# Attention of layer 0: the sums of the keys turned by four transposes and added on VectorE, the last sample's outputs turned in another PSUM bank, and the second sample's input loaded three steps later

## The chip, the cores and the metric

The kernel runs on one core of a Trainium2 chip. The metric is the device time in microseconds. TensorE does the matmuls and transposes, VectorE and ScalarE (ACT in the profile, VectorE is DVE) the elementwise work, GpSimd (POOL) some setup, and SyncE (SP) issues most DMA transfers. [...]

## The reference

Two layers work on x of shape 4 x 128 x 64 x 64. Only layer 0 is touched by the change; layer 1 (an attention with eight heads over 4096 tokens and a layer of 64 experts) follows it in the same kernel.

```python
e1 = _conv1x1(x, w1, b1, a1).reshape(N, -1, HW)     # x is the group-normed input
e2 = _conv1x1(x, w2, b2, a2).reshape(N, -1, HW)
asm = _conv1x1(x, wa, ba, aa).reshape(N, C, HW)
score = jnp.einsum('nci,ncj->nij', e1, e2)
score = jax.nn.softmax(score, axis=2)
out = jnp.einsum('nij,ncj->nci', score, asm)
x = x + out
```

So for each of four samples there are 4096 queries and 4096 keys of 64 channels and values of 128 channels. All of it is fp32.

## The kernel before, in words

Layer 0 goes through the samples b, in each through eight blocks qb of 512 queries, and in each block through 16 steps p of two key chunks of 128. A list `steps` holds the 512 steps in order. `probs` of a step multiplies keys and queries into a PSUM tile `sc` (two buffers), has ACT write the exponentials `pr` (three buffers), and has VectorE add them into `acc`, which so collects, for each query, the sum over the keys of each partition. `weigh` multiplies `pr` with the values into two PSUM tiles `av`. The scores of a step are issued two steps ahead of its weighing.

Behind a block's last step comes its tail. `collect` adds the two `av` tiles into `o` and the two halves of `acc` into `sums` (a single buffer). The rest is done for the block before, called `done`: `row_sums` sums `sums` over the partitions, that is over the keys, with four small matmuls against a column of ones into the PSUM tile `pd`, copies the result to `rows` and takes the reciprocal `inv`; `finish` turns `o` by four transposes into the PSUM tile `otr`, and VectorE scales it with `inv`, adds the input `xr` and writes the tokens `t`. Between `row_sums` and `finish` TensorE gets other work: in samples 0 to 2 the projections (`project`, tile `pe`, and `value`, tile `pa`) of the next sample; in the last sample the transposes of layer 1's tokens (`tokens`, tile `f_ltr`, copied by ACT to `f_ama`) and, from block 1 to 6, layer 1's four key chunks (`keys`, tile `f_pk`). In the last sample some steps of layer 1's scan (tile `f_ur` and others) are put there too by `point()`.

PSUM tiles with the same tag share a bank: `pd` and `pa` use bank `sm`; `pe`, `f_ltr`, `f_ur` and `otr` use bank `x`. A tile in a bank waits until the readers of the tile before it have finished.

TensorE's instructions keep the order in which the program writes them. In layer 0 the order on VectorE, ACT, POOL and SP is decided when the program is built, by priorities and estimated times, so an operation written at one place can stand elsewhere in its engine's queue. The input of a sample, `x`, has a single buffer: the load of the second sample can start when the first sample's last normalization (`normal`) has read it. It consists of four transfers on SP, and the statistics (`stat`, line 1923) of the second sample read it. Those same queues carry, for each chunk of the projection, the transfers `e<-e` and `e<-side`, which TensorE's scores need.

`tile_stats` and `close_stats` take the LayerNorm statistics of the sample before on VectorE (lines 256 and 257) and its root on ACT (line 260).

## Time and profile before

| what | us |
|---|---|
| median of three runs | 2300.96 (2299.47 to 2301.77) |
| the profiled execution | 2302.78 |
| its span, from the first to the last instruction | 2301.0 |
| TensorE busy | 2237.1 |
| VectorE busy | 1448.4 |
| ACT busy | 1092.1 |
| POOL busy | 174.8 |

Layer 0 fills about the first 1530 us of the span. One step takes 2.57 us there; in the middle of a sample a block takes 44.9 us, in the last sample about 51.7. A line of the profile's timeline gives the start, the duration, the engine, the line of the source, the operation and its tiles, how many like instructions were merged, and in brackets how long the engine was idle before it and what ended that. PE is TensorE's matmuls, PEld its weight loads. An fp32 matmul is two records (two passes), a transpose is one.

### The profile page before, as it was taken

To read this page: it belongs to the slowest core of one execution; us is meant where nothing else is said; L and a number is where in the kernel's file an instruction comes from. 1 tells how busy PE (TensorE), PEld (TensorE's weight loads), DVE (VectorE), ACT (ScalarE), POOL (GpSimd) and SP (SyncE) were. 2 spreads that over 40 slices of the span, in tenths; PEclk is the share of its full clock that TensorE was granted. 3 is DMA by queue.
4 is the path that set the end of the run, shared out by engine and by line. 5 is a ranking of instruction groups with operands and counts; after the bars stand their busy time and mean duration, and the time that the engine had idled before them with its cause. 6 is when DMAs were issued, how large, how long until landed. Compare 5 with 4: busy or idle time off the path is not lost.

```text
span 2301.0 us, 43192 instructions
## 1 busy us (share of the span) xinstructions
PE 2237.1 (97%) x18352; PEld 1161.9 (50%) x18352; DVE 1448.4 (63%) x2380; ACT 1092.1 (47%) x1328; POOL 174.8 (8%) x380
## 2 busy tenths in 40 slices
PE   7999999999999999999999999999999999999997
PEld 3544444444444444444444444456556555666663
DVE  7666565655666565556555666567867777775643
ACT  2343334433333443344445454445566666565651
POOL 0000000000000000000000000021221221223311
PEclk9999999999999999999999999999999999999999
DMA  2100010000010000001000000010211211323588
GB/s 75 34 12 17 9 45 9 17 9 9 11 52 9 9 17 9 9 9 44 9 5 5 5 5 10 5 50 25 64 46 39 65 53 41 94 55 113 170 301 331
DMA packets 79419, 108.96 MB, mean 47 GB/s; under 512 B 9072, under 2 KB 44912, under 8 KB 78960
## 3 DMA queue, kind: packets, MB, share of 16 engines
q1 hardware_dynamic: 78128, 104.01, 14.5%
q8 instruction: 146, 2.39, 0.4%
q0 software_dynamic: 512, 1.05, 0.2%
q10 hardware_dynamic: 576, 1.05, 0.1%
q14 instruction: 57, 0.47, 0.1%
HBM read 80.64 MB, written 19.14 MB: 43 GB/s over the span
## 4 chain that ended last, share of the span: by engine, by line
PE 88%; DVE 6%; ACT 3%; DMA 2%; issue 1%; SPq 0%; ACTq 0%; DVEq 0%
PE av L2033 37%; PE sc L2008 18%; PE f_pv L1130 9%; PE f_pk L975 8%; PE f_pt L1153 3%; PE f_po L1176 2%; PE pd L2059 1%; PE f_po L1188 1%; ACT f_e1a L982 1%; PE pa L1981 1%; PE pe L1955 1%; DMA x<-in_x_dram 1%; DVE f_e1a L983 1%; DVE f_e1a L984 1%; PE f_pl L1296 1%
## 5 line engine op out<-in xcount | busy, mean ns | idle before, releaser
L2033 PE MATMUL av<-pr,am 64*128 64x512 f32 x4096 | 978.0, 592 | 1.9 <-ACT pr L2013 1.8
L2013 ACT ACTIVATE pr<-sc 128x1024 f32<-128x1024 f32 x512 | 524.2, 1024 | 781.2 <-PE sc L2008 767.7
L2020 DVE TENSOR_TENSOR acc<-acc,pr 128x1024 f32<-128x1024 f32 x480 | 586.7, 1222 | 485.4 <-ACT pr L2013 481.1
L2033 PEld LDWEIGHTS av<-pr,am 64*128 64x128 f32 x4096 | 401.7, 187 | 471.7 <-issue 458.0
L2008 PE MATMUL sc<-e,e 64*128 64x512 f32 x2048 | 534.7, 591 | 4.8 <-DMA e<-side 4.8
L2008 PEld LDWEIGHTS sc<-e,e 64*128 64x128 f32 x2048 | 201.6, 187 | 237.0 <-issue 229.2
L1130 PE MATMUL f_pv<-f_held,f_ama 128*32 128x256 f32 x4096 | 239.3, 382 | 6.2 <-ACT f_e1a L982 5.1
L975 PE MATMUL f_pk<-f_held,f_ama 128*128 128x512 f32 x512 | 235.0, 603 | 0.0
L1135 ACT ACTIVATE f_amb<-f_pv 128x1024 f32<-128x1024 f32 x128 | 131.0, 1025 | 132.3 <-PE f_pv L1130 131.3
L983 DVE TENSOR_TENSOR f_e1a<-f_e1a,f_held 128x1024 f32<-128x1024 f32 x128 | 157.6, 1232 | 47.8 <-ACT f_e1a L982 47.6
L982 ACT ACTIVATE f_e1a<-f_pk 128x1024 f32<-128x1024 f32 x128 | 129.8, 1025 | 110.0 <-PE f_pk L975 56.7
L1130 PEld LDWEIGHTS f_pv<-f_held,f_ama 128*32 128x32 f32 x4096 | 129.7, 110 | 101.7 <-issue 12.4
L984 DVE TENSOR_REDUCE f_e1a<-f_e1a 128x8 f32<-128x1024 f32 x128 | 155.3, 1218 | 3.5
L975 PEld LDWEIGHTS f_pk<-f_held,f_ama 128*128 128x128 f32 x512 | 92.5, 190 | 108.3 <-issue 101.0
L1094 POOL COPY f_held<-f_e1a 32x32 f32<-32x32 f32 x128 | 30.7, 240 | 911.1 <-DVE f_e1a L1076 565.8
L1153 PE MATMUL f_pt<-f_amb,f_held 128*32 128x128 f32 x1920 | 83.2, 276 | 0.8 <-ACT f_amb L1135 0.8
L920 POOL MEMSET f_held<- 128x1024 f32 x1 | 1.0, 957 | 1035.2 <-DVE xn L1946 1035.2
L1153 PEld LDWEIGHTS f_pt<-f_amb,f_held 128*32 128x32 f32 x1920 | 60.0, 109 | 10.4 <-issue 5.2
L1194 DVE TENSOR_TENSOR t<-t,f_po 128x512 f32<-128x512 f32 (+1 forms) x33 | 22.1, 672 | 56.0 <-PE f_po L1188 56.0
L958 ACT ACTIVATE f_xl<-t,ln_nb,ln_rs 128x128 f32<-128x128 f32 x128 | 52.8, 491 | 0.8 <-PE pa L1981 0.8
L1277 ACT ACTIVATE f_x<-t,f_gnb,f_grs 128x128 f32<-128x128 f32 x122 | 49.7, 482 | 0.4 <-DVE f_gnb L1256 0.4
L2017 DVE COPY acc<-pr 128x1024 f32<-128x1024 f32 x32 | 22.2, 694 | 39.3 <-ACT pr L2013 39.3
(304 smaller groups left out, 1792.9 us busy)
## 6 DMA issues: line engine op xcount, KB each, us to landing
f_e2a<-f_rd SPq DMA_DIRECT2D x128, 128.0 KB, 3.1
xr<-in_xtok_dram SPq DMA_DIRECT2D x32, 256.0 KB, 2.6
f_table<-f_x SPq DMA_DIRECT2D x62, 128.0 KB, 2.2
out_dram<-t SPq DMA_DIRECT2D x14, 512.0 KB, 5.0
x<-in_x_dram SPq DMA_DIRECT2D x12, 512.0 KB, 4.5
e<-e SPq DMA_DIRECT2D x32, 128.0 KB, 2.2
f_ama<-f_rd SPq DMA_DIRECT2D x16, 256.0 KB, 4.0
f_e1b<-f_rd SPq DMA_DIRECT2D x16, 256.0 KB, 3.9
```

The lines of the kernel that those rows point to most:

```text
L958: nc.scalar.activation(xl[:, c, :], t[:, b * NCH + i, :], AF.Identity, bias=ln_nb[:, b, i : i + 1], scale=ln_rs[:, b, i : i + 1],)
L975: nc.tensor.matmul(pk[:, i, :], xt_at(n)[:, bass.ts(c, P)], env.wks[:, bass.ts(i, BLK)], start=True, stop=True,)
L982: nc.scalar.activation(flat, pk.rearrange("p i x -> p (i x)"), AF.Silu)
L983: nc.vector.tensor_mul(ks, ks, env.qb)
L984: nc.vector.tensor_reduce(s[:, (n % GB) * CPB + c, :], ks, AX.X, ALU.add)
L1130: nc.tensor.matmul(pv[a * CH : (a + 1) * CH, i, :], xt_at(m)[:, bass.ts(c * NA + i, CH)], env.wvs[:, bass.ts(a, HH * C)], start=True, stop ...
L1135: nc.scalar.activation(env.amb[:, bass.ts(c, HD)], pv.rearrange("p i x -> p (i x)"), AF.Silu)
L1153: nc.tensor.matmul(env.pt[i * CH : (i + 1) * CH, :], lhs, rhs, start=i not in env.begun, stop=False, skip_group_check=True,)
L2008: nc.tensor.matmul(sc[:, u, :], e2[halves[u], p, :], e1[halves[u], cols], start=True, stop=True,)
L2013: nc.scalar.activation(pr, sc, AF.Exp)
L2020: nc.vector.tensor_add(acc, acc, pr)
L2033: nc.tensor.matmul(av, am[h, j, :], pr[h, u, :], start=(j == 0), stop=(j == NCH - 1))
```

## The change

`collect` is split: the addition of the two halves of `acc` becomes `add_keys`, which is called behind `row_sums` of the block before. `row_sums` turns the four 128-query parts of `sums` with transposes into a whole bank, and VectorE adds over the keys in one reduction. `finish` gets the tag of its PSUM tile as an argument: bank `sm` in the last sample, bank `x` otherwise and for the very last block. The load of the second sample is called at step 13 of the first block instead of at step 10, where the last chunk is projected.

```diff
                 def collect(b, qb):
                     lower, upper_ = av_of.pop((b, qb))
-                    o = tmp.tile([P, BLK], F32, tag="o", name=f"o_{b}_{qb}")
+                    o_of[b, qb] = o = tmp.tile([P, BLK], F32, tag="o", name=f"o_{b}_{qb}")
                     nc.scalar.copy(o, lower)
                     nc.vector.tensor_add(o, o, upper_)
+
+                def add_keys(b, qb):
+                    o = o_of[b, qb]
                     acc = acc_of.pop((b, qb))
                     sums = tmp.tile([P, BLK], F32, tag="sums", name=f"sums_{b}_{qb}", bufs=1)
                     nc.vector.tensor_add(sums, acc[:, 0, :], acc[:, 1, :])
...
                 def row_sums(b, qb):
...
-                    pd = ps.tile([P, BLK], F32, tag="sm", name=f"pd_{b}_{qb}")
+                    pd = ps.tile([P, CPB, P], F32, tag="sm", name=f"pd_{b}_{qb}")
                     for c in range(CPB):
-                        nc.tensor.matmul(
-                            pd[:, c : c + 1], sums[:, bass.ts(c, P)], ones, start=True, stop=True
-                        )
-                    nc.vector.tensor_copy(rows[:, at], pd[:, :CPB])
+                        nc.tensor.transpose(pd[:, c, :], sums[:, bass.ts(c, P)], ident)
+                    nc.vector.tensor_reduce(rows[:, at], pd, AX.X, ALU.add)
...
-                def finish(b, qb):
+                def finish(b, qb, tag="x"):
...
-                    ptr = ps.tile([P, CPB, C], F32, tag="x", name=f"otr_{b}_{qb}")
+                    ptr = ps.tile([P, CPB, C], F32, tag=tag, name=f"otr_{b}_{qb}")
...
-                        if k == NBLK - 1:
-                            xs_of[1] = load_x(1)
+                    if n == NPR - 3:
+                        xs_of[1] = load_x(1)
...
                         collect(b, qb)
                         if done:
                             row_sums(*done)
+                        add_keys(b, qb)
...
                         if done:
-                            finish(*done)
+                            finish(*done, "sm" if b == B - 1 else "x")
```

## The prediction

> **What bounds the kernel now.** I read the page's first part, then the chain of waits, the groups with shapes kept apart, the list of TensorE's waits in layer 0, and the timeline at several block ends.

> ```profile
> PE 2237.1 (97%) x18352; PEld 1161.9 (50%) x18352; DVE 1448.4 (63%) x2380; ACT 1092.1 (47%) x1328; POOL 174.8 (8%) x380
> PE 88%; DVE 6%; ACT 3%; DMA 2%; issue 1%; SPq 0%; ACTq 0%; DVEq 0%
> ```

> TensorE is busy 97% of the span and is 88% of the chain: an edit counts by what it adds to or takes from TensorE's own sequence. VectorE (63%) has room on average, but it is crowded just behind a block's end, where this change puts its work.

> ```profile
> L984 DVE TENSOR_REDUCE f_e1a<-f_e1a 128x8 f32<-128x1024 f32 x128 | 155.3, 1218 | 3.5
> ...
> L2059 PE MATMUL pd<-ones,sums 128*128 128x1 f32 x256 | 33.6, 252 | 0.0
> ...
> L2044 DVE TENSOR_TENSOR sums<-acc 128x512 f32<-128x512 f32 x32 | 22.2, 692 | 16.3 <-PE pd L2059 16.2
> ...
> L2071 PE MATMUL otr<-ident,o 128*128 128x128 f32 x128 | 19.7, 276 | 8.6 <-ACT f_ama L968 6.9 <-ACT y L1957 1.1 <-DVE f_e1a L995 0.6
> ```

> Columns: busy us, mean ns of one, idle before it and its cause. The four row-sum matmuls of a block are 8 records (256 for 32 blocks), its four transposes are 4. The means (252, 276) include latency that overlaps the next record, so cost is read from start to start in the timeline of one tail, the stretch between two blocks (T = 174.88, where pd starts):

> ```profile
> 174.88 1.05 PE L2059 MATMUL pd<-ones,sums 128*128 128x1 f32 x8
> ...
> 175.79 1.10 PE L1955 MATMUL pe<-xn,w 128*128 128x512 f32 x2
> 175.97 0.69 DVE L2044 TENSOR_TENSOR sums<-acc 128x512 f32<-128x512 f32 x1 [0.54 <-PE pd L2059]
> 176.58 0.15 DVE L2062 COPY rows<-pd 128x4 f32<-128x4 f32 x1
> ...
> 176.88 1.13 PE L1981 MATMUL pa<-was,xn 128*128 128x128 f32 x8
> ...
> 177.84 0.60 PE L2071 MATMUL otr<-ident,o 128*128 128x128 f32 x4
> ...
> 178.37 1.99 PE L2033 MATMUL av<-pr,am 64*128 64x512 f32 x8
> ```

> TensorE goes from pd to pe in 0.91 us (T+0.91), starts pa at T+2.00, otr at T+2.96 and the next av at T+3.49. The four otr transposes hold it 0.53 us. On VectorE the sums wait for pd to have read the old sums (16.2 us over the run), and pa, which takes pd's bank, starts just after the rows copy has ended (176.73).

> **What the change costs, part by part.**

> *Row sums by transposes (32 blocks).* Removed: 8 records, 0.91 us. Added: 4 transposes of otr's kind. I take 0.55 us (0.53 after pa; 0.58 in the row of 1221.50 below, where they start cold). So pe starts at T+0.55 and its two passes, 0.43 each, end at T+1.41. [...]

> *The sum on VectorE.* A 128x4 copy (0.155) becomes a reduction of 128x512 from PSUM, which the trace does not have. Nearest rows: o, 128x512 reading PSUM, 0.69; and L984, a reduction of 1024 elements in 1218 ns, no slower than the add of that size (1222). I take 0.69; bounds 0.6 and 1.2. It can start at T+0.70 (o, which ran from 174.74, ends T+0.55; the transposes' last record ends T+0.66), ends T+1.39, and pa follows 0.12 to 0.15 later as it now follows the copy: T+1.54 against T+2.00. **Gain of a plain tail: 0.46 us.** Otr's bank waits for y, which ends at T+2.4 (pe's end T+1.65 plus ACT's 0.69), as pa ends: covered, by almost nothing. VectorE's order changes too: reduction, acc, reciprocal, sums, instead of sums, copy, reciprocal, acc. Sums no longer wait for TensorE; acc needs the pr that ACT ends at T+1.13. By start spacings (0.61, 1.11, 0.16, 0.61) z begins at T+3.19 instead of T+3.09. VectorE is therefore 0.1 later in absolute time and 0.56 later against TensorE. Where a step's probabilities (3 buffers) are awaited with slack that costs nothing; behind z wait e, side, t, statistics and the next acc, and at five tails TensorE waits for one of these:
> - the tail at 126.4 with two projections (otr waited 1.1 us for y, which waited for VectorE's e): -0.1.
> - the two with an x load and its statistics (VectorE waits for the DMA until 324.4; av waits at 331.84): -0.1 each.
> - the two at 446 and 807, where the LayerNorm root stands between two exponentials on ACT. There the built order puts the acc addition ahead of the last aggregate instead of behind it (the order of VectorE's queue in both programs shows it):

> ```profile
> 455.03 0.30 DVE L257 BATCH_NORM_AGGREGATE ln_mv<-l_st 128x2 f32<-128x6 f32 x2
> 455.25 1.19 DVE L2020 TENSOR_TENSOR acc<-acc,pr 128x1024 f32<-128x1024 f32 x1
> 455.37 0.32 ACT L260 ACTIVATE ln_rs<-ln_mv,eps 128x32 f32<-128x32 f32 x1 [0.61 <-DVE ln_mv L257]
> ...
> 458.08 1.99 PE L2033 MATMUL av<-pr,am 64*128 64x512 f32 x8 [0.55 <-ACT pr L2013]
> ```

> The root waits for the aggregate, av (458.08) for the exponential after the root. Spacing 1.11 plus 0.1, less rounding: -1.15 each.

> Samples 0 to 2 have 23 such tails: 18 x 0.46 = 8.3, less 0.1, 0.2 and 2.3: **+5.7 us**.

> *Last sample's outputs in bank sm.* Now they share bank x with the tokens' transposes and wait until ACT has copied these out:

> ```profile
> 1219.65 0.60 PE L967 MATMUL f_ltr<-ident,f_xl 128*128 128x128 f32 x4
> ...
> 1220.86 0.58 ACT L968 COPY f_ama<-f_ltr 128x512 f32<-128x512 f32 x1
> ...
> 1221.50 0.66 PE L2071 MATMUL otr<-ident,o 128*128 128x128 f32 x4 [1.25 <-ACT f_ama L968]
> ...
> 1222.08 1.99 PE L2033 MATMUL av<-pr,am 64*128 64x512 f32 x8
> ```

> ```profile
> PE otr L2071 <- ACT f_ama L968: 6.9, 6, 1.2
> PE sc L2008 <- DMA e<-side: 4.8, 3, 2.1
> ```

> Otr could have started 0.44 after ltr, and started 1.85 after it: 1.40 lost. In bank sm it waits for the reduction instead, done 5 us earlier because four key chunks lie between. By block:
> - 0: TensorE gains 0.7, but pr of step 2 then comes behind a LayerNorm root that waits for t on VectorE: -0.1.
> - 1 to 4: 0.36 + 1.40 = 1.76 earlier; pr of step 2 ended 1.1 us before its use (1226.23, used 1227.34) and moves only 0.36 with the keys, so 0.35 comes back as a wait: 1.41 each, 5.6.
> - 5 (no normals on ACT there): 1.76.
> - 6: f_ur in bank x still waits for the copy; the wait behind it goes: 1.13.
> - 7: no keys lie between. Otr now waits for the reduction, which stands behind o on VectorE (1526.03 to 1526.72): ends 1527.34, otr at 1527.46 instead of 1526.22: -1.24. The final row sums, behind it: +0.33.

> Sum **+7.5 us**. POOL's setup waits for the last t, about 1.4 later; TensorE is 0.9 later there, and POOL is next needed at 1545: covered by 4 us.

> *The clock.* One stretch of 3.5 us at half clock stands right behind block 6's tail:

> ```profile
> 1479.60:1483.10 3.50, 1.66 (x13) 0.94 (x11) 3.45 (x5) 3.17 (x4) 0.00 (x0) 1.00 0.00 0
> 1483.10:1486.60 3.50, 3.50 (x10) 1.48 (x12) 3.50 (x7) 0.55 (x1) 0.00 (x0) 0.52 0.00 0
> ```

> The row of 1479.60 has TensorE busy 1.66 of 3.50 us; the next has the clock at 0.52. [...] Tails of 2.4 us without a matmul (blocks 1 to 5) drew no dip; this one, 3.4, did. With the change it is 2.6: **+1.7 us**. [...]

> *Second x loaded three steps later.* At no cost and no gain. The order of instructions on SP's queue is the same in both programs: the four x transfers still stand behind the sixth chunk's side transfer and ahead of the seventh chunk's e and side, waiting for the same VectorE step; the statistics of x stand at the same place on VectorE. No queue is passed; POOL's and SP's orders are identical. The 4.8 us that sc waits for e<-side stay.

> Sum: 5.7 + 7.5 + 1.7 = 14.9 us. The profiled execution took 2302.8 (span 2301.0, 1.8 around it): 2287.9, span 2286.1. The median shown, 2300.96, lies 1.8 below the profiled time; less 14.9 it is 2286. After 1531 TensorE is 98 to 99% busy until 2100 and the weights' loads start from rooms it frees, so the shift is carried to the end.

> **Rivals.**
> 1. *The bank is slow (no change).* The reduction takes 1.2 us, L984's figure. Then pa starts at T+2.05: 18 x -0.05; the five special tails -5.1; last sample +6.0; clock +1.7: gain 1.8, 2299. Serial transposes (1.10 us) end near 2301. For: no row reduces from PSUM. Against: o's 0.69 does read PSUM.
> 2. *VectorE's queue decides (slower).* One mechanism: the reduction holds bank sm before pa and stands ahead of acc. [...] It decides from about 1.25 us on. Against: nothing of 128x512 on VectorE takes over 0.7 here.
> 3. *The x load does move.* If its statistics leave the seventh chunk's path, the 4.8 us go as well: 2281. Against: identical orders.
> 4. *The change does little at the plain tails*, because y or z decide otr or the next steps: their 0.46 becomes 0.2: 2291. It is in the forecast's range.

> **Numbers.** Forecast with rival 4: 0.80, gains of 9 to 20. Rival 3: 0.06. Rival 1: 0.08, no change. Rival 2: 0.06. Within 0.2% (4.6 us) is about what a measurement of this kernel can't tell from no change. Faster 0.86, same 0.08, slower 0.06. Range 2280 to 2294: low end, transposes at 0.44 and no lag on ACT (+21); high end, rival 4 with no clock gain and one more lag of 1 us per root (+7); it leaves out rivals 1 and 2.

> **What would show it.** Right: pd's four records in 0.6 us, pe at T+0.55, reduction near 0.69, pa at T+1.5; otr's 6.9 us wait for f_ama gone, a new wait of about 1.2 for rows at block 7; longer av waits for pr (from 1.8 to about 5); no clock dip near 1480; e<-side still 4.8. Wrong: a reduction over 1 us, pa later than T+1.9, exponentials waiting for acc in every tail, or new half-clock stretches in layer 0.

## The result

| | before | after |
|---|---|---|
| median | 2301.36 us (2298.48 to 2303.56, 6 runs) | 2288.24 us (2285.81 to 2288.86, 6 runs) |
| ratio after to before | | 0.994, 95% interval 0.9929 to 0.995 |
| span of the profiled execution | 2301.0 | 2287.0 |
| TensorE busy | 2237.1 | 2223.4 |
| VectorE busy | 1448.4 | 1460.2 |

The changed kernel is faster by 13.1 us by the medians; 14.9 were forecast. The interval of the ratio means 11.5 to 16.3 us. The end of layer 0 (the last `pd`) comes at 1517.42 us instead of 1530.13, 12.7 us earlier, of the 14.0 by which the profiled span is shorter: nearly all of the gain is made in layer 0, where the change is.

First the page's busy times, then two of the edited lines from the groups with shapes kept apart (busy us, mean ns of one, idle before it and its cause), after the change:

```profile
PE 2223.4 (97%) x18224; PEld 1147.4 (50%) x18224; DVE 1460.2 (64%) x2380; ACT 1091.6 (48%) x1328; POOL 175.9 (8%) x380
```

```profile
L2063 DVE TENSOR_REDUCE rows<-pd 128x4 f32<-128x512 f32 x32 | 22.1, 692 | 7.1 <-PE pd L2062 2.7
...
L2072 PE MATMUL otr<-ident,o 128*128 128x128 f32 x128 | 19.4, 274 | 2.8 <-DVE rows L2063 1.8 <-ACT y L1957 1.0
```

TensorE has 128 records fewer, VectorE 11.8 us more. The reduction, which the trace of before did not have, takes 692 ns, as the forecast took from `o` (0.69). The outputs' transposes wait 2.8 us instead of 8.6, and no longer for `f_ama`. The chain of waits of this profile consists of one piece of 0.01 us and tells nothing; TensorE's share of the span, still 97%, stands for it here.

A plain tail in the timeline of the changed kernel (T = 176.61, the same tail that the prediction shows at 174.88):

```profile
176.61 0.66 PE L2062 MATMUL pd<-ident,sums 128*128 128x128 f32 x4
...
177.11 1.02 PE L1955 MATMUL pe<-xn,w 128*128 128x512 f32 x2
177.31 0.69 DVE L2063 TENSOR_REDUCE rows<-pd 128x4 f32<-128x512 f32 x1
177.91 1.22 DVE L2020 TENSOR_TENSOR acc<-acc,pr 128x1024 f32<-128x1024 f32 x1
...
178.05 1.16 PE L1981 MATMUL pa<-was,xn 128*128 128x128 f32 x8
...
179.05 0.60 PE L2072 MATMUL otr<-ident,o 128*128 128x128 f32 x4
...
179.58 1.99 PE L2033 MATMUL av<-pr,am 64*128 64x512 f32 x8
```

From `pd` to `pe` it is 0.50 us (0.91 before), `pa` starts at T+1.44 (T+2.00), `otr` at T+2.44 (T+2.96), the next `av` at T+2.97 (T+3.49). The reduction starts as the transposes end and ends at T+1.39; `pe` holds TensorE until about then as well (its two passes of 0.43 end at T+1.36), so there is next to nothing left between `pe` and `pa`.

In the last sample the tail that the prediction shows at 1219.65 now reads:

```profile
1215.92 0.60 PE L967 MATMUL f_ltr<-ident,f_xl 128*128 128x128 f32 x4
...
1216.36 0.60 PE L2072 MATMUL otr<-ident,o 128*128 128x128 f32 x4
...
1217.14 0.58 ACT L968 COPY f_ama<-f_ltr 128x512 f32<-128x512 f32 x1
```

`otr` follows 0.44 behind `f_ltr` instead of 1.85, ahead of the copy that it used to wait for. At the last block, where no key chunks lie between, it waits instead for the reduction, which stands behind `o`:

```profile
1512.15 0.69 DVE L2041 TENSOR_TENSOR o<-o,av 128x512 f32<-128x512 f32 x1 [1.75 <-ACT o L2040]
1512.75 0.68 DVE L2063 TENSOR_REDUCE rows<-pd 128x4 f32<-128x512 f32 x1
...
1513.49 0.66 PE L2072 MATMUL otr<-ident,o 128*128 128x128 f32 x4 [1.41 <-DVE rows L2063]
```

TensorE's waits in layer 0 (the first 1535 us; total us, times, longest) after the change:

```profile
PE av L2033 <- ACT pr L2013: 8.1, 10, 2.2
PE sc L2008 <- DMA e<-side: 3.9, 2, 2.1
...
PE otr L2072 <- DVE rows L2063: 1.8, 2, 1.4
```

The 6.9 us for `f_ama` are gone, 1.8 for `rows` are new. The waits of `av` for the exponentials grew from 1.8 to 8.1, more than the 5 foreseen. Half of the growth is at the two LayerNorm-root tails, where the wait is 2.15 instead of 0.55; this is the one at 805.17 (T):

```profile
814.25 1.19 DVE L2020 TENSOR_TENSOR acc<-acc,pr 128x1024 f32<-128x1024 f32 x1
...
815.36 0.17 DVE L257 BATCH_NORM_AGGREGATE ln_mv<-l_st 128x2 f32<-128x6 f32 x1
815.57 0.32 ACT L260 ACTIVATE ln_rs<-ln_mv,eps 128x32 f32<-128x32 f32 x1 [2.21 <-DVE ln_mv L257]
815.91 1.28 ACT L2013 ACT_TABLE_LOAD   x1
...
817.20 1.94 ACT L2013 ACTIVATE pr<-sc 128x1024 f32<-128x1024 f32 x2
...
818.28 1.89 PE L2033 MATMUL av<-pr,am 64*128 64x512 f32 x4 [2.15 <-ACT pr L2013]
```

The `acc` addition stands ahead of the last aggregate, so the root comes at T+10.40 instead of the T+9.33 of before, and behind it a table load of 1.28 us, the exponential and `av`. TensorE waits 2.15 us. What the clock does there, in windows of the same trace (length, busy us of PE, PEld, DVE, ACT, POOL with counts, then the granted clock as a share of full speed, 0.50 being half; the last two columns are the DMA's; the last two windows lie around block 6's tail of the last sample):

```profile
815.10:818.52 3.42, 1.27 (x8) 0.43 (x6) 1.24 (x5) 2.92 (x4) 0.00 (x0) 1.00 0.01 3
818.52:821.93 3.41, 3.41 (x10) 1.39 (x10) 2.19 (x2) 0.62 (x1) 0.00 (x0) 0.50 0.00 0
...
1467.05:1470.47 3.42, 2.17 (x11) 0.98 (x10) 3.37 (x4) 2.07 (x3) 0.00 (x0) 1.00 0.00 0
1470.47:1473.88 3.41, 3.41 (x18) 1.67 (x18) 3.41 (x6) 1.78 (x3) 0.00 (x0) 1.00 0.00 0
```

The half clock behind block 6's tail is gone, as forecast; behind the root's wait there is a new one.

### The profile page after: what moved, and what is told of

Its sections match the earlier page's. It is cut to its first block, busy times and chain, and to the rows that moved or that the text cites. A ratio compares the mean times of both kernels' runs of the same rounds, so it can differ in the third digit from the quotient of the medians.

```text
span 2287.0 us, 42915 instructions
## 1 busy us (share of the span) xinstructions
PE 2223.4 (97%) x18224; PEld 1147.4 (50%) x18224; DVE 1460.2 (64%) x2380; ACT 1091.6 (48%) x1328; POOL 175.9 (8%) x380
## 3 DMA queue, kind: packets, MB, share of 16 engines
q0 software_dynamic: 512, 1.05, 0.2%
q10 hardware_dynamic: 576, 1.05, 0.1%
## 5 line engine op out<-in xcount | busy, mean ns | idle before, releaser
L2033 PE MATMUL av<-pr,am 64*128 64x512 f32 x4096 | 980.0, 593 | 8.1 <-ACT pr L2013 8.1
L2013 ACT ACTIVATE pr<-sc 128x1024 f32<-128x1024 f32 x512 | 523.9, 1025 | 779.4 <-PE sc L2008 763.4
L2020 DVE TENSOR_TENSOR acc<-acc,pr 128x1024 f32<-128x1024 f32 x480 | 587.4, 1224 | 472.3 <-ACT pr L2013 468.7
L2033 PEld LDWEIGHTS av<-pr,am 64*128 64x128 f32 x4096 | 402.1, 187 | 480.3 <-issue 455.7
L2008 PE MATMUL sc<-e,e 64*128 64x512 f32 x2048 | 536.7, 593 | 3.9 <-DMA e<-side 3.9
L2008 PEld LDWEIGHTS sc<-e,e 64*128 64x128 f32 x2048 | 202.7, 188 | 236.5 <-issue 230.9
L984 DVE TENSOR_REDUCE f_e1a<-f_e1a 128x8 f32<-128x1024 f32 x128 | 155.3, 1218 | 3.5
L2017 DVE COPY acc<-pr 128x1024 f32<-128x1024 f32 x32 | 22.2, 694 | 39.3 <-ACT pr L2013 39.3
```

The lines of the kernel that those rows point to most:

```text
L984: nc.vector.tensor_reduce(s[:, (n % GB) * CPB + c, :], ks, AX.X, ALU.add)
L2008: nc.tensor.matmul(sc[:, u, :], e2[halves[u], p, :], e1[halves[u], cols], start=True, stop=True,)
L2013: nc.scalar.activation(pr, sc, AF.Exp)
L2020: nc.vector.tensor_add(acc, acc, pr)
L2033: nc.tensor.matmul(av, am[h, j, :], pr[h, u, :], start=(j == 0), stop=(j == NCH - 1))
```

## The experiments

In every kernel of the study the time from one tail's `pd` to the next was read from the trace and compared with the same tail of before. That difference repeats to 0.01 to 0.02 us at most tails, so single traces are compared tail by tail, and the total only by the ratios. A tail is named by its place in before (446 is the one at 446 us); minus is shorter than before. The columns are the changed kernel, the same once more, each of its parts alone, and two repaired kernels; each is described below. The ratios are to before as it ran beside each kernel (medians of 2301.98 to 2303.04 us).

| tails | after | again | sums alone | bank alone | load alone | stats early | both repairs |
|---|---|---|---|---|---|---|---|
| 18 plain, each | -0.53 | -0.53 | -0.53 | 0.00 | 0.00 | -0.53 | -0.53 |
| root at 446 | +1.08 | +2.77 | +2.77 | 0.00 | +0.01 | -0.06 | -0.06 |
| root at 807 | +2.76 | +2.76 | +2.76 | 0.00 | 0.00 | -0.07 | -0.07 |
| x load at 309 | -0.44 | +0.77 | +0.62 | -0.66 | +0.03 | +0.58 | +0.84 |
| x load at 671 | +1.20 | +0.73 | +1.07 | +0.67 | +1.00 | +0.37 | +0.09 |
| last sample, blocks 1 to 4, each | -1.45 | -1.45 | -0.51 | -0.96 | 0.00 | -1.46 | -1.45 |
| block 5 | -1.97 | -1.97 | -0.50 | -1.47 | 0.00 | -1.97 | -1.97 |
| block 6, with the clock | -2.87 | -2.87 | -2.20 | -2.36 | -0.06 | -2.86 | -2.87 |
| block 7 | +1.17 | +1.17 | -0.45 | +1.30 | +0.01 | +1.17 | -0.46 |

| kernel | median us | ratio to before, 95% interval |
|---|---|---|
| sums alone | 2294.69 | 0.9964 (0.9952 to 0.9975) |
| bank alone | 2296.05 | 0.9973 (0.9966 to 0.9981) |
| load alone | 2301.22 | 0.9991 (0.9981 to 1.0001) |
| stats early | 2285.67 | 0.992 (0.9902 to 0.9937) |
| last output in x | 2289.39 | 0.9937 (0.9919 to 0.9954) |
| sums ahead of the reduction | 2325.01 | 1.0095 (1.0073 to 1.0118) |
| two reductions | 2322.9 | 1.0084 (1.006 to 1.0108) |
| both repairs | 2280.42 | 0.9906 (0.9891 to 0.9921) |
| both repairs, shared buffers | 2302.19 | 1.0002 (0.9993 to 1.001) |

### Each part alone

Sums alone: the changed kernel with the other two parts taken back.

```diff
-                            finish(*done, "sm" if b == B - 1 else "x")
+                            finish(*done)
-                    if n == NPR - 3:
-                        xs_of[1] = load_x(1)
+                        if k == NBLK - 1:
+                            xs_of[1] = load_x(1)
```

> The kernel before with the row sums by transposes and the split addition alone (outputs of the last sample stay in bank x, second x load at its old place). If the parts add up as in the prediction: the 18 plain tails of samples 0 to 2 gain 0.53 us each as in the changed kernel (9.5), the special tails give back about 3, and each tail of the last sample keeps only the 0.4 to 0.5 that TensorE is earlier at pd (about 3), with otr still waiting 1.2 us for f_ama; half clock near 1480 stays. About 2301.3 - 9.9 = 2291. Rival (most of the gain is the change of bank): a gain under 5 us, 2297 or more, because pa or the next steps wait for VectorE.

Measured: 0.9964, some 8 us. Every plain tail gains the same 0.53; the special tails of samples 0 to 2 behave as in the changed kernel; in the last sample each block keeps about 0.5, and `otr` waits the old 6.9 us for `f_ama` (6 times). The half clock near 1480, which was expected to stay, is absent from this profile (block 6: -0.50 and -1.70). The edit did not shorten the pause in which it arose: from the start of `f_ltr` to the start of the next `av` it is 3.41 us in both kernels. Before:

```profile
1479.62 0.60 PE L967 MATMUL f_ltr<-ident,f_xl 128*128 128x128 f32 x4
...
1483.03 3.59 PE L2033 MATMUL av<-pr,am 64*128 64x512 f32 x8
```

Sums alone:

```profile
1474.69 0.60 PE L967 MATMUL f_ltr<-ident,f_xl 128*128 128x128 f32 x4
...
1478.10 1.99 PE L2033 MATMUL av<-pr,am 64*128 64x512 f32 x8
```

What differs is where the pause lies among the steps of 3.413 us in which the half-clock stretches begin; the last section shows it. The rival falls.

Bank alone: the kernel before with the tile's tag.

```diff
-                            finish(*done)
+                            finish(*done, "sm" if b == B - 1 else "x")
```

> The kernel before with the last sample's outputs turned in bank sm, nothing else. Prediction's theory: samples 0 to 2 are unchanged; otr's wait for f_ama (6.9 us) goes, tails of blocks 1 to 4 gain about 1.05 each, block 5 1.4, block 6 0.8, block 7 loses 1.2 (otr waits for rows), and the half clock near 1480 goes, 1.7: together 5.4 to 7.1 us, 2294 to 2296. Rival (the next exponentials take the place of the wait): under 3 us.

Measured: 0.9973, some 6 us. Samples 0 to 2 are the same to 0.01 us except at the x loads. Blocks 1 to 4 gain 0.96 each: the `av` behind `otr` comes 1.47 earlier, and 0.5 of it comes back at a later `av`, which waits for its exponential. Block 7 loses 1.30. At blocks 1 to 5 the two parts add up to the whole (0.51 + 0.96 = 1.47 against 1.45; 0.50 + 1.47 = 1.97).

Load alone: the kernel before with the call moved.

```diff
-                        if k == NBLK - 1:
-                            xs_of[1] = load_x(1)
+                    if n == NPR - 3:
+                        xs_of[1] = load_x(1)
```

> The kernel before with the second x load called at step 13 instead of step 10, nothing else. Theory: no difference (all queues carry the same instructions in the same order), 2301 within 1 us, e<-side still about 4.8 us. Rival (the statistics leave the seventh chunk's path): 2296.5, e<-side gone. What moves in this profile is run-to-run: the place of half-clock stretches and the time of the x transfers.

Measured: 0.9991, an interval that holds 1; e<-side 4.0 us. The rival, which wanted it gone, falls. Because this kernel has before's queues, its trace is also a measure of what wanders by itself: the tail at 671 is 1.00 longer than in the other profile of the same order, half clock costs 1.70 us at 1170, and there are two stretches of it before the first tail.

The changed kernel once more:

> The changed kernel once more, for what repeats. If the loss of 1.2 us at the second sample-boundary x load (682.9) and the half-clock stretches at 34, 82 and 830 are run-to-run, they move or go here; if they come from the change's order of instructions, they stay at the same tails. Plain tails 0.53 shorter than before again, time 2286 to 2289.

Measured, one run: 2290.01 us. The half clock at the root tail of 807 stays, at the other root tail it appears now (2.77 instead of 1.08), and the loss at 671 becomes 0.73 with +0.77 at 309. So the root tails' loss belongs to the change. The x loads' moves between executions of one kernel, as the next reading shows.

At a tail with an x load, VectorE's statistics wait for the transfers. The tail at 671 in the changed kernel's profile, and the same second pair before:

```profile
682.91 1.29 DVE L1923 BATCH_NORM_STATS2 stats<-x 128x6 f32<-128x512 f32 x2 [3.59 <-DMA x<-in_x_dram]
684.58 1.28 DVE L1923 BATCH_NORM_STATS2 stats<-x 128x6 f32<-128x512 f32 x2 [0.39 <-DMA x<-in_x_dram]
```

```profile
685.77 1.29 DVE L1923 BATCH_NORM_STATS2 stats<-x 128x6 f32<-128x512 f32 x2 [0.67 <-DMA x<-in_x_dram]
```

The second pair starts at T+15.63, and the tail's period (from its `pd` to the next) is 46.46. In before it is T+14.43 and 45.26. In all 20 such tails of ten traces, those of the two kernels with a late reduction left out, the period is this start plus 30.82 or 30.83, with or without the change. The start itself runs from T+14.16 to T+15.67. The four transfers are issued from T+8.2 to T+9.7 in both kernels; when they land decides these tails, not the tail's work. Whether the change also moves the landing is open: the two tails together stand at 0.0 and +1.0 in the kernels with before's sums, at +0.2 to +1.7 in those with the new ones, too few readings with such a scatter to tell.

### Is it the end of the reduction that lets `pa` start?

Two kernels make the reduction end later. In the first the addition of the two halves of `acc` is called where it was before:

```diff
                         collect(b, qb)
+                        add_keys(b, qb)
                         if done:
                             row_sums(*done)
-                        add_keys(b, qb)
```

> The changed kernel with the addition of the two halves of acc called ahead of the row sums, as before the change; VectorE's order is then o, sums, acc, reduction. Theory (the end of the reduction sets pa's start): sums waits for pd and ends at T+1.3, acc follows to T+2.4, the reduction ends at T+3.1, pa starts at T+3.2 instead of T+1.44, so a plain tail is about 1.8 longer than in the changed kernel, 1.3 longer than before: 18 x 1.8 = 32 us and some 7 at the special tails, about 2320 to 2328, slower than before. Rival (pa is set by pe or y, and the reduction has slack): 2288 to 2292.

A plain tail in its timeline (T = 502.20):

```profile
502.20 0.66 PE L2062 MATMUL pd<-ident,sums 128*128 128x128 f32 x4
...
502.89 0.69 DVE L2047 TENSOR_TENSOR sums<-acc 128x512 f32<-128x512 f32 x1
503.50 1.22 DVE L2020 TENSOR_TENSOR acc<-acc,pr 128x1024 f32<-128x1024 f32 x1
...
504.63 0.68 DVE L2063 TENSOR_REDUCE rows<-pd 128x4 f32<-128x512 f32 x1
...
505.47 1.13 PE L1981 MATMUL pa<-was,xn 128*128 128x128 f32 x8 [1.75 <-DVE rows L2063]
```

`pa` starts at T+3.27, 0.16 behind the reduction's end, and each plain tail is 1.27 longer than before, 1.80 longer than in the changed kernel. Measured 2325.01 us, 1.0095: 22 us slower than before, with the changed kernel's instructions. The rival falls. So splitting the addition off is no side matter; it puts the reduction at the head of VectorE's row.

In the second the reduction is issued twice.

```diff
                     nc.vector.tensor_reduce(rows[:, at], pd, AX.X, ALU.add)
+                    nc.vector.tensor_reduce(rows[:, at], pd, AX.X, ALU.add)
```

> The changed kernel with the reduction issued twice, the second time over the first: what a reduction of twice the duration would do. Theory: pa starts 0.6 to 0.69 later, T+2.1, which is 0.1 later than before the change; 18 plain tails lose 0.65 each (11.7), the special ones 0.65 to 1, block 7 0.65: 15 to 17 us more than the changed kernel, 2303 to 2305, no gain or a small loss against before. Rival (slack in front of pa): under 5 us.

Measured 2322.9 us, 20 more than the kernel before, where 2303 to 2305 were expected. The timeline of a plain tail (T = 499.98) says why:

```profile
500.67 0.69 DVE L2063 TENSOR_REDUCE rows<-pd 128x4 f32<-128x512 f32 x1
501.28 1.21 DVE L2020 TENSOR_TENSOR acc<-acc,pr 128x1024 f32<-128x1024 f32 x1
...
502.41 0.68 DVE L2064 TENSOR_REDUCE rows<-pd 128x4 f32<-128x512 f32 x1
...
503.24 1.13 PE L1981 MATMUL pa<-was,xn 128*128 128x128 f32 x8 [1.75 <-DVE rows L2064]
```

The built order put the second reduction behind `acc`, so this is not a reduction of twice the duration but one that ends 1.7 later, and the test of a 1.4 us reduction stays open. The relation is the same: `pa` at T+3.26 is 1.26 later than before, the tail 1.27 longer. With the changed kernel (0.56 earlier, 0.53 shorter) `pa`'s start and the tail's length move together at all three places.

### The order at the LayerNorm root

The last block's statistics of samples 0 and 1 are written right behind that block's outputs, with buffers of their own. On VectorE the last aggregate then stands ahead of `xn` and `acc` at the two root tails; every other queue has the changed kernel's order.

```diff
-                    if b > 0 and 2 <= qb < 6 and p % 2 == 0:
+                    if b > 0 and 2 <= qb < 6 and p % 2 == 0 and (qb, p) < (5, 8):
                         tile_stats(tmp, b - 1, (qb - 2) * NBLK + p // 2)
...
                             finish(*done, "sm" if b == B - 1 else "x")
+                            if b > 0 and qb == 0:
+                                for i in range(NCH - CPB, NCH):
+                                    st = tmp.tile([P, 6], F32, tag="l2_st", name=f"l2_st_{b}_{i}", bufs=4)
+                                    nc.vector.bn_stats(st, t[:, (b - 1) * NCH + i, :])
+                                    nc.vector.bn_aggr(ln_mv[:, b - 1, i, :], st)
```

> The changed kernel with the statistics of the last block of samples 0 and 1 written right behind that block's outputs, so that at the two LayerNorm-root tails (446 and 807) the last aggregate stands ahead of the acc addition again and nothing else moves on any engine. If the order of aggregate and acc is the cause there, the root comes 1.1 us earlier, TensorE's 2.15 us of waiting shrinks to about 1.0, and the 1.7 us of half clock behind it go too: each of the two tails falls from 1.1 or 2.8 above before to about 0.0, together 2.2 to 5.6 us, about 2284 to 2286 where the changed kernel gives 2288 to 2290. Rival (it is VectorE's delay of 0.6 us as such): 1.2 us at most, half clock stays.

The root tail at 802.64 in its timeline:

```profile
811.69 0.17 DVE L2160 BATCH_NORM_AGGREGATE ln_mv<-l_st 128x2 f32<-128x6 f32 x1
811.78 1.19 DVE L2020 TENSOR_TENSOR acc<-acc,pr 128x1024 f32<-128x1024 f32 x1
811.90 0.32 ACT L260 ACTIVATE ln_rs<-ln_mv,eps 128x32 f32<-128x32 f32 x1 [1.08 <-DVE ln_mv L2160]
...
814.61 0.70 PE L2033 MATMUL av<-pr,am 64*128 64x512 f32 x2 [1.01 <-ACT pr L2013]
```

The root is back at T+9.26, TensorE waits 1.01 instead of 2.15, and no half clock follows. The two tails stand at -0.06 and -0.07: the order cost 1.14 each, and the half clock 1.70 more wherever the trace showed it (at 807 in the changed kernel, its repeat, the sums alone and the last output in x; at 446 in the repeat and the sums alone only). Measured 2285.67 us, 0.992, as expected; this interval overlaps the changed kernel's, so here too the tails settle it.

### The last block, and both repairs

```diff
-                            finish(*done, "sm" if b == B - 1 else "x")
+                            finish(*done, "sm" if b == B - 1 and qb < NBLK - 1 else "x")
```

> The changed kernel with the outputs turned at the end of the last sample's last block left in bank x, as before; blocks 0 to 6 stay in bank sm. Theory: otr waits no longer for the reduction there, the last tail of layer 0 is 1.2 to 1.7 shorter (from 1.17 above before to 0.45 below, as in the kernel with the sums alone), about 1.5 us less in all. Rival: the wait is hidden by what follows (row sums of the last block), then no change.

In its timeline `otr` follows `pd` without a wait, and the tail goes from +1.17 to -0.46:

```profile
1510.52 0.66 PE L2062 MATMUL pd<-ident,sums 128*128 128x128 f32 x4
...
1511.01 0.60 PE L2072 MATMUL otr<-ident,o 128*128 128x128 f32 x4
```

The median, 2289.39, does not show these 1.63 us: the interval of its ratio (0.9919 to 0.9954) contains the changed kernel's. From its last `pd` to the end the profile has 776.6 us, against 769.6 in the changed kernel; half-clock stretches with TensorE at work come to 13.7 us there instead of 10.2, which is 1.7 of these 7.0; the rest was not followed. The total alone would not have settled this edit, the tail does.

> The changed kernel with both repairs: last aggregates ahead of acc at the two LayerNorm-root tails, and the last block's outputs back in bank x. If the repairs add up: 1.14 + 2.83 us at the two tails and 1.63 at the end of layer 0, 5.6 less than in the changed kernel, about 2283 to 2285 beside before at 2302; no half clock in samples 1 and 2. If one hides the other, 2285.5 or more.

Measured 2280.42 us, 0.9906 (0.9891 to 0.9921). The repairs add up in layer 0, and this interval lies below the changed kernel's: the version is faster than the changed kernel and than before. It is 2.6 below the low end of what was expected; in its profile the first tail comes 1.8 earlier than in the changed kernel's, and the time from the last `pd` to the end is 2.3 shorter, neither of which the repairs touch. TensorE's longest wait of `av` for an exponential is 1.0 us in its profile.

The last kernel differs only in that the early statistics share the four buffers of the others:

```diff
-                                    st = tmp.tile([P, 6], F32, tag="l2_st", name=f"l2_st_{b}_{i}", bufs=4)
-                                    nc.vector.bn_stats(st, t[:, (b - 1) * NCH + i, :])
-                                    nc.vector.bn_aggr(ln_mv[:, b - 1, i, :], st)
+                                    tile_stats(tmp, b - 1, i)
```

> As the kernel with both repairs, but the last block's statistics share the four buffers of the other statistics: the built order then puts all statistics of a sample behind the last block's outputs, in one row at the two tails, and out of the six tails before; the root comes one step later. If the statistics behind a plain tail cost nothing (theory: its steps have slack), only the two tails differ, and the longer row of statistics there (28 more of 0.4 us) makes VectorE late: 0 to 6 us more than with both repairs, 2284 to 2290. If the statistics did crowd the tails with the x load, those two get up to 1 us shorter each and it is the faster of the two.

Measured 2302.19 us, as slow as before the change, where 2284 to 2290 were expected. Shared buffers are taken in the program's order, so the 28 earlier statistics now stand behind the last block's. The plain tails are still at -0.53, so the statistics had cost them nothing, but the tails at 446, 807 and 1167 are 6.3 to 6.7 longer than before. Two rows of its timeline, the root and the `av` behind it, at the first of them:

```profile
464.10 0.32 ACT L260 ACTIVATE ln_rs<-ln_mv,eps 128x32 f32<-128x32 f32 x1 [5.50 <-DVE ln_mv L257]
...
466.81 3.78 PE L2033 MATMUL av<-pr,am 64*128 64x512 f32 x8 [5.43 <-ACT pr L2013]
```

The root stands ahead of the exponential on ACT and waits for all the statistics, and TensorE waits with it, 5.43 us. Behind each of these three waits the trace has 6.8 us of half clock, which is part of the loss.

## Why the prediction was right, point by point

The mechanisms forecast for the row sums, the bank, the roots' order and the x load are the ones that the experiments show. The clock's term is not, and that the sum still came within 2 us of the measured gain is in part luck, as the point on the clock says.

**Row sums.** Forecast: `pe` 0.36 earlier (0.91 less 0.55), reduction 0.69 and ended at T+1.39, `pa` at T+1.54, 0.46 gained. Measured: 0.41, 0.692, T+1.39, T+1.44, 0.53. The mechanism held; the terms that were mis-sized are the transposes' pitch (0.50 instead of 0.55) and the lag from the reduction's end to `pa`, 0.05 by the records instead of 0.12 to 0.15 (it is 0.15 where TensorE has been idle for 1.75 us, as in the two kernels with a late reduction). Over 18 tails that is 9.5 us instead of 8.3. In the changed kernel `pe` and the reduction end within 0.03 us of each other, so which of the two sets `pa` there can't be told; it is the reduction once that comes late. Counting from start to start was right, against the row's mean (276 ns before, 274 after) paid one after the other: four transposes cost 0.50 us, not 1.10, and 0.41 us is saved of the 0.91 of before. Rivals 1 and 4 fall with this.

**VectorE's queue.** Rival 2 wanted a reduction that ends late. It did not, but the two kernels above show that the rival's mechanism is real: a reduction that ends 1.7 us later makes the kernel 20 to 22 us slower than before.

**The special tails.** The double projection: a gain of 0.06, forecast a loss of 0.1. The two roots by order: a loss of 1.08 and 1.06, forecast 1.15; shown by the kernel with the early statistics. What the forecast left out is the clock: the longer wait there draws 1.7 us of half clock, at one root in this profile and at both in its repeat. The two x loads: forecast a loss of 0.1 each, measured -0.44 and +1.20, where kernels with before's queues spread by 0.7 and 1.0; the landing of x decides. The sum over samples 0 to 2 in this trace is a gain of 5.0 us (9.5 + 0.1 + 0.4 - 1.1 - 2.8 - 1.2), forecast 5.7.

**Last sample.** Forecast by block: -0.1 for block 0 (a gain of 0.02), 1.41 each for blocks 1 to 4 (1.45), 1.76 for block 5 (1.97), 1.13 for 6 (1.17 without the clock), a loss of 1.24 for 7 (1.17). The final row sums go from 0.81 to 0.44 between `pd` and `otr`, a gain of 0.37, forecast 0.33. Together 8.2 against 7.5. All eight signs but block 0's hold, and the give-back at blocks 1 to 4, which the bank alone shows as 0.5.

**The clock.** Forecast: the stretch near 1480 goes, +1.7. With the outputs in the other bank it is gone in all nine profiles; the pause there, from the start of `f_ltr` to the next `av`, is 2.74 us in the changed kernel instead of 3.41. It stayed in load alone, and in the sums alone it is absent though the pause is as long as before. The sum counted only the stretch that went, and took it for a fixed cost of the kernel before. That the length of the pause decides was the author's estimate; no run shows such a length: a wait of 2.15 us had half clock behind it in six of eight cases, the pause of 3.41 in two of three. New half-clock stretches in layer 0, which the prediction lists among the signs that it is wrong, did come: the one behind the root at 807, and two before the first tail, where both kernels have the same queues, where load alone has the same two and six other profiles have one. The first tail comes 1.79 later in this profile. So the step that failed is "The clock" as a net gain: in this profile it is +1.7 at block 6, -1.7 at the root, and the rest is run to run. Over many executions it is, by estimate, a loss. By the steps of the last section and the 1.65 us read there from the traces, the old pause at block 6 would draw half clock in some 40% of the positions that the steps can have (1.35 of 3.41 us), and each root's wait in some 60% (2.04 of 3.41). If every position is as likely, that is 0.7 us lost before and 2.0 after, so -1.4 in place of the forecast's +1.7. The plain tails (1.2) and the last sample (0.7) came out better than forecast, and made up for most of these 3.1 us.

**The x load.** Forecast nothing: 0.9991 with an interval that holds 1, the waits for e<-side 3.9 us here and 4.0 in load alone. Rival 3 falls.

**The sum.** Up to the last `pd`: samples 0 to 2 5.0, last sample 7.8 ahead of the final row sums, clock 1.7, less 1.8 at the start: 12.7, as the trace has it. Forecast 14.9 with the final 0.33. The difference lies in the root's half clock and the start, partly paid by better plain tails and a better last sample.

## What to carry to other kernels

When an operation in a shared bank grows, ask what stands ahead of it on the engine that empties the bank: here the reduction at the head of VectorE's row took 0.53 us off each plain tail, and behind two additions it put 1.27 on. A built order can flip two neighbours that the edit never touched (an aggregate and an addition), and that cost more than some of the edit's own terms; compare the queues, then give the flipped operation its own place and buffers. Where totals wander by some us, compare stage by stage: the same tail repeats to 0.02 us. A half-clock stretch seen in one profile can be a chance, not a fixed cost (behind the wait at the root of 446 it came in two of four profiles): before counting on it, see in how many profiles it comes.

## What was not expected of the hardware

A wait of TensorE of 2.15 us behind a stretch of full work drew half clock in all of four profiles at one place and in two of four at another, while 0.55 and 1.0 us at the same places drew none. A stretch costs 1.7 us (1.69 at the root of 446, +2.77 against +1.08; 1.70 at 1170 in load alone).

Windows that are such steps (the columns as above; the busy time of PE comes first, the clock behind POOL). The pause at block 6's tail before, and in the sums alone:

```profile
1479.86:1483.27 3.41, 1.57 (x12) 0.88 (x12) 3.36 (x4) 3.34 (x4) 0.00 (x0) 1.00 0.00 0
1483.27:1486.68 3.41, 3.41 (x10) 1.39 (x10) 3.41 (x7) 0.38 (x1) 0.00 (x0) 0.50 0.00 0
```

```profile
1475.51:1478.92 3.41, 1.79 (x10) 1.00 (x12) 3.36 (x5) 3.19 (x4) 0.00 (x0) 1.00 0.00 0
1478.92:1482.34 3.42, 3.42 (x18) 1.55 (x16) 3.42 (x9) 1.02 (x1) 0.00 (x0) 1.00 0.00 0
```

The changed kernel: the two steps around the wait at the root of 446, and block 7's tail (the step of the wait at 807 stands in the section on the result, at 815.10):

```profile
453.29:456.70 3.41, 2.37 (x12) 0.77 (x8) 2.32 (x9) 1.58 (x2) 0.00 (x0) 1.00 0.26 77
456.70:460.12 3.42, 2.31 (x12) 1.13 (x14) 2.23 (x2) 1.97 (x3) 0.00 (x0) 1.00 0.00 0
...
1511.41:1514.82 3.41, 2.00 (x12) 1.30 (x11) 2.58 (x7) 1.87 (x2) 0.00 (x0) 1.00 0.10 38
```

At 446 a step ends inside the wait and splits it, and no half clock follows; so it is in the last output in x, the other of the four without one. In the six cases with half clock the wait lies within one step (816.13 to 818.28 at the root of 807 in the changed kernel, in the step from 815.10 to 818.52). At block 7's tail the transposes of `pd` and `otr` are 1.31 us of the 2.00: other matmuls fill less than a microsecond of that step, less than the 1.27 at 815.10, where no transpose runs, and no half clock follows (the clock of the next step is 1.00).

Half-clock stretches outside the edited part differ from one profile to the next: after 1510 us, those that begin while TensorE still works sum to 3.4 us (both repairs, with and without shared buffers, and the repeat of the changed kernel) and up to 13.7 us (four kernels, among them bank alone and last output in x), 1.7 to 6.8 us of lost time.

A reduction of 128x512 that reads PSUM takes as long as an addition that reads a PSUM tile of the same size (692 ns against 0.69 us), and the statistics that wait for the transfers of x begin with a scatter of 1.5 us at the same issue time.
